# A graph-attention layer with the features as weights and the attention moving

## The chip, the cores and the metric

The kernel runs on one core of one Trainium2 chip. The metric is the device time of one execution in microseconds (us): the median of three runs of the kernel before. One further execution was taken with the hardware profiler; its trace is the source of every duration below. TensorE is called PE in the profile (PEld is its weight load), VectorE DVE, ScalarE ACT, GpSimd POOL, SyncE SP.

## What is computed

Four residual layers run over `x` of 32 batches x 512 nodes x 64 features, float32, with one 512x512 adjacency matrix `adj` for all batches. Each layer starts with `h = max(layernorm(x), 0)`:

- layer 0: `x += h Ws + (adj h) Wn + bias`
- layer 1: twice `z = relu((adj z) W_i)`, then `x += z`
- layer 2, graph attention, which the change is about:

```python
Wh = einsum('bnf,of->bno', h, W)
e1 = Wh @ a[:F_OUT]
e2 = Wh @ a[F_OUT:]
e = leaky_relu(e1[:, :, None] + e2[:, None, :], negative_slope=0.2)
att = softmax(where(adj > 0, e, -9e15), axis=-1)
x += elu(einsum('bij,bjo->bio', att, Wh))
```

- layer 3: attention with eight heads and an output layer of the same kind (`gat_layer`), again added to `x`.

## The kernel before

**Stages.** `x` stays on the chip, in 128 partitions of 4 blocks of nodes (C = 4, P = 128, F = 64). Layers 0, 1 and 2 are done in one software pipeline over M = 16 pairs of batches: a slot `k` (function `slot`) does layer 0 of pair k, layer 1 of pairs k-1 to k-3 and layer 2 of pairs k-3 to k-5. Seventeen slots run, then `drain` finishes the last four pairs of layer 2. After that layer 3 runs in periods of its own (`planned`), with other buffers; `drain` already starts its first features (`flow_period(-10)` to `(-2)`).

**Order.** For these layers the order of the instructions on TensorE, VectorE and ScalarE is exactly the order in which the code issues them (`manual_schedule`); each engine works through its own list and waits where something is missing. So what matters is what stands ahead of what in each list.

**Layer 2 of a pair** (class `Gat`) uses that exp(leaky_relu(e1 + e2)) is, up to a factor of the row that the softmax cancels, `max(exp(-0.8 e1), exp(0.8 e2)) * exp(0.2 e2)`.

- `flip` turns the normalised features with TensorE; `prepare` multiplies them by the weights (`wh_ps`, lines 960 to 971, with e2 as a 65th column) and makes e1 as a row in all partitions (`e1_ps`, L974); ScalarE takes the exponentials: into the last column of `v`, `q`, and `c` (L983 to L986).
- `weigh` (L991) multiplies the features by exp(0.2 e2) into `v`: 64 features and one column that will give the denominator.
- `scores` (L1000): VectorE makes `s = max(c, q) * mask`, eight instructions of 128x512 per pair, in two halves, four and four.
- `values` (L1014): TensorE multiplies, with `s` as weights and `v` (65 columns) as what moves. A block of `s` holds 64 neighbours of each of the two batches, one batch in partitions 0 to 63 and one in 64 to 127, so a product uses half the rows of the array, and the two halves go side by side. Per pair 4 x 8 x 2 = 64 products. A float32 product has two records in the trace, so 128 records; a transposition has one.
- `read` (L1029, L1030): VectorE takes the reciprocal of the 65th column and multiplies, straight from PSUM, into `o`.
- `rest`: ScalarE takes exp(o) (L1038), VectorE adds both parts of the elu to `x` (L1041, L1042), computes the mean and centres for layer 3's norm (L861 to L863), and ScalarE squares (L1044).

`end` is `read` and then `rest`.

**What stands around it in a slot.** TensorE's list at the end of a slot and the beginning of the next: `values`; the two projections of layer 0 (`po0`, L941); the second neighbour product of layer 1 (`nt1b`, L921); `judge`'s small transposition in slot 15; then, next slot, the first neighbour product of layer 1 (`nt1`, L921, of `hn`); `flip`; the projection `po1b` (L941), which needs the copy of `nt1b` by ScalarE (L928); layer 0's transposition and neighbour product; `prepare`; the projection `po1a`; `values`. ScalarE's list at that turn: exp(o) L1038, the square L1044, the copy of `nt1b`, the square of a norm (L881), the copies of `nt1` and of the flipped features (L312). VectorE's: the reciprocals of the norms and relu (L914, L885), then in some slots extra work (`begun`: `judge_rows`, seven instructions that judge one block of rows of the adjacency matrix, L201 to L213, in slots 6, 8, 10, 12; `judge` in slot 15; `edges`, which makes the mask, in slot 1; `scales`, in slot 4), then `read` and `rest`, then layer 0's addition to `x` (L1097), the next norms, `scores`.

The norms' spreads are summed by VectorE (L899) and turned into roots by ScalarE (`root`, L906), ahead of relu.

**Drain.** The pairs are called g2, g1, g0 and last. Products that lead nowhere (`fill`, L1168) stand in TensorE's list between the stages.

**Buffers.** `ps_t` has four PSUM buffers for everything tagged `ps`; `ps_g` two, for the `acc` of `values`; `ps_o` two, for projections.

Of the kernel before, what the change touches and what calls it, by code (L numbers as in the profile page):

```python
# [8 lines left out]
F32 = mybir.dt.float32  # L9
AF = mybir.ActivationFunctionType  # L10
OP = mybir.AluOpType
# [11 lines left out]
def fast_form(  # L23
# [201 lines left out]
    def halves(k):  # L225
        return slice(k * F, (k + 1) * F)

    def row_pair(name):

        return pairs_of[0].tile([P, 2, N], F32, name=name, tag="row")  # L230
# [611 lines left out]
    with (  # L842
# [107 lines left out]
        class Gat:  # L950
# [8 lines left out]
            def prepare(self):  # L959


                self.wh_ps = [
                    ps_t.tile([P, C, F + 1], F32, name="wh_ps", tag="ps") for b in range(2)
                ]
                for b in range(2 * C):
                    for k in range(2):
                        nc.tensor.matmul(
                            self.wh_ps[b // C][halves(k), b % C],
                            lhsT=self.ht[halves(k), b * F : (b + 1) * F],
                            rhs=wgv[halves(k), :], start=True, stop=True,  # L970
                        )
                e1 = ps_t.tile([P, N], F32, name="e1_ps", tag="ps")
                for k in range(2):
                    nc.tensor.matmul(  # L974
                        e1[halves(k), :], lhsT=wa1[halves(k), :F], rhs=self.ht[halves(k), :],
                        start=True, stop=True,
                    )
                self.v = work.tile([P, 2 * C, F + 1], F32, name="v")
                self.q = tiny.tile([P, 2 * C], F32, name="q")
                for b in range(2):  # L980
                    e2 = self.wh_ps[b][:, :, F]
                    some = slice(b * C, (b + 1) * C)
                    nc.scalar.activation(self.v[:, some, F], e2, AF.Exp, scale=0.2)  # L983
                    nc.scalar.activation(self.q[:, some], e2, AF.Exp, scale=0.8)
                self.c = row_pair("c")[:, 0]
                nc.scalar.activation(self.c, e1, AF.Exp, scale=-0.8)  # L986

            def weigh(self):
                for b in range(2):
                    v = self.v[:, b * C : (b + 1) * C]  # L990
                    nc.vector.tensor_tensor(  # L991
                        v[:, :, :F], self.wh_ps[b][:, :, :F],
                        v[:, :, F:].to_broadcast([P, C, F]), OP.mult,
                    )

            def scores(self, part):

                self.s = getattr(self, "s", []) + [row_pair("s") for b in range(C // 2)]
                for b in range(part * C, (part + 1) * C):
                    nc.vector.scalar_tensor_tensor(  # L1000
                        self.s[b // 2][:, b % 2], self.c, self.q[:, b : b + 1],
                        mask_t[b // C][:, b % C], op0=OP.max, op1=OP.mult,
                    )

            def values(self, rows=range(C)):

                if 0 in rows:
                    self.acc = [
                        ps_g.tile([P, C, F + 1], F32, name="acc") for k in range(2)
                    ]  # L1010
                for r in rows:
                    for b in range(2 * C):
                        for k in range(2):
                            nc.tensor.matmul(  # L1014
                                self.acc[k][:, r],
                                lhsT=self.s[b // 2][halves(k), b % 2, r * P : (r + 1) * P],
                                rhs=self.v[halves(k), b],
                                start=(b == 0), stop=(b == 2 * C - 1),
                            )

            def end(self):
                self.read()
                self.rest()

            def read(self):
                rec = tiny.tile([P, 2, C], F32, name="rec")
                self.sq = o = work.tile([P, 2, C, F], F32, name="o")
                for k in range(2):
                    nc.vector.reciprocal(rec[:, k], self.acc[k][:, :, F])  # L1029
                    nc.vector.tensor_tensor(  # L1030
                        o[:, k], self.acc[k][:, :, :F],
                        rec[:, k, :, None].to_broadcast([P, C, F]), OP.mult,
                    )

            def rest(self):
                o = self.sq
# [49 lines left out]
        def slot(k, more):  # L1086
            l0, l1 = 0 <= k < M, 0 <= k - 2 < M
            if l0:
                x2 = pair_of(k).rearrange("p k c f -> p (k c) f")
                nc.gpsimd.tensor_tensor(  # L1090
                    x2, x2, bias0_b[:, None, :].to_broadcast([P, 2 * C, F]), OP.add
                )
            if k - 3 in nt1b:
                nt1b[k - 3] = copied(nt1b[k - 3], "nt1b")
            if k - 1 in po0:
                x4 = pair_of(k - 1)
                nc.vector.tensor_tensor(  # L1097
                    x4, x4, po0.pop(k - 1).rearrange("p c k f -> p k c f"), OP.add
                )
            some = []  # L1100
            n = make(n1, k - 1)
            if n:
                n.a()
                n.square()
                some.append(n)
            if l1:
                h = n1.pop(k - 2).h
                nt1 = copied(neighbours(lambda c: h[:, c]), "nt1")
            if k - 4 in n2:
                gat[k - 4] = Gat(k - 4, n2.pop(k - 4).h)  # L1110
                gat[k - 4].flip()
            u = gat.pop(k - 5, None)
            if u:
                u.scores(0)
            if k - 3 in nt1b:
                ends(k - 3)
            if l0:
                h0 = n0.pop(k).h
                ht0 = flipped(h0, "ht0")
            n = make(n2, k - 3)  # L1120
            if n:
                n.a()
                n.square()
                some.append(n)
            if l0:
                nt0 = copied(neighbours(lambda c: h0[:, c]), "nt0")
            if u:
                u.scores(1)
            if k - 4 in gat:
                gat[k - 4].prepare()  # L1130
            if l1:
                z = middle(nt1)
            n = make(n0, k + 1)
            if n:
                n.a()
                n.square()
                some.append(n)
            some += ended
            ended.clear()
            s = Spread()  # L1140
            for n in some:
                s.add(n)
            if u:
                u.values()
            s.root()
            if k - 4 in gat:
                gat[k - 4].weigh()
            s.turn()
            for n in some:
                if isinstance(n, Gat):  # L1150
                    flow_stats[n.i] = n.mean, n.rstd
                else:
                    n.relu()
            if l0:
                po0[k] = project([(ht0, ws2), (nt0, wn2)], "po0")
            if l1:
                nt1b[k - 2] = neighbours(lambda c: z[:, c, :])
            if more:
                more()
            if u:  # L1160
                u.end()
# [8 lines left out]
        def drain():  # L1170
# [19 lines left out]
            s.add(u)  # L1190
            s.root()
            nt1b[M - 1] = copied(nt1b[M - 1], "nt1b")
            g2.values(range(C // 2))
            g1.weigh()
            s.turn()
            n.relu()
# [3 lines left out]
            n = make(n2, M - 1)  # L1200
            n.a()
            n.square()
            g2.values(range(C // 2, C))
            g1.scores(0)
            g0.flip()
            g2.read()
# [4 lines left out]
            s.add(n)  # L1211
            s.root()
            g1.values()
            s.turn()
            n.relu()
            last = Gat(M - 1, n2.pop(M - 1).h)
# [6 lines left out]
            g0.scores(1)  # L1223
            fill(6)
            g0.values()
            last.weigh()
            g1.rest()
            last.scores(0)
# [5 lines left out]
            last.scores(1)  # L1234
            fill(3)
            last.values()
            g0.rest()
            s.add(g1)
            last.read()
# [7 lines left out]
                flow_stats[n.i] = n.mean, n.rstd  # L1247


        mask_t = [  # L1250
            setup.tile([P, C, N], F32, name=f"mask{b}", tag=("raw", "mask")[b])
            for b in range(2)
        ]

        def edges():
            for b in range(2):
                for k in range(2):
                    blocks = mask_t[b][:, k::2]
                    nc.vector.tensor_scalar(
                        blocks[halves(k)], adj_t[halves(k), b * C // 2 : (b + 1) * C // 2],  # L1260
                        0.0, None, op0=OP.is_gt,
                    )
                    nc.sync.dma_start(blocks[halves(1 - k)], blocks[halves(k)])

        with tc.manual_schedule(
            engines={
# [609 lines left out]
```

## Time and profile before

| what | value |
|---|---|
| median of three runs | 2043.86 us (2043.75 to 2046.07) |
| the profiled execution's own time | 2045.32 us |
| its span in the trace | 2043.5 us |
| mean granted TensorE clock | 0.989 |
| PE busy 100 to 350 us | all of it |
| `values` of layer 2 (L1014), all 16 pairs | 2048 records, 124.0 us busy |
| its weight loads | 2048, 121.0 us busy |
| layers 0 to 2, end | 454 us (first product of layer 3's scores) |

How to read it: the profile's page has a line per engine, the span cut into 40 slices with the busy tenths of each engine and the granted clock (`PEclk`), and groups of instructions. A group's line gives line, engine, operation, output and inputs, the shape of the tile of the array (rows*columns) and of what moves, the count, then busy time and the mean duration in ns, then the idle time of the engine just before and what ended it. A line of the order of time gives the start, the length (to the modelled end), the engine, the line of code, the operation and its shapes, the count of instructions merged, and in brackets the idle time ahead of it with the engine and result that ended it. TensorE's instructions overlap, so the difference of two starts tells the pace and a duration does not.

### The profile page before, as it was taken

The page shows a single profiled execution, that of the slowest core. Times are in us where ns is not written, and L with a number is a line of the kernel's source. Part 1 is how long each engine was busy: PE and PEld are TensorE (multiplying, and loading weights), DVE is VectorE, ACT ScalarE, POOL GpSimd, SP SyncE. Part 2 cuts the span into 40 slices and gives each one's busy share as a digit, 9 for nine tenths or more (in the row PEclk, how much of TensorE's full clock was granted, in tenths as well). Part 3 has the DMA queues.
Part 4 walks back from the last instruction along what each step waited for, and adds up shares of the span by engine and source line. Part 5 has one row for each costly group of instructions (what it writes and reads, how often), then busy time and mean ns, then how long its engine had stood idle before and what let it go on. Part 6 is the DMA issues. An engine that isn't in the chain of part 4 may idle for free.

```text
span 2043.5 us, 32571 instructions
## 1 busy us (share of the span) xinstructions
PE 1980.7 (97%) x11038; PEld 811.0 (40%) x11038; DVE 1753.4 (86%) x4121; ACT 1295.2 (63%) x1960; POOL 1445.8 (71%) x834
## 2 busy tenths in 40 slices
PE   7999999997999999999999999999999999999995
PEld 4676676762333333333333333333333333333332
DVE  6699996768988899889898898888898898888984
ACT  3443443346677777777677777676676776766674
POOL 2000000006898989899999989898888988889996
PEclk9999999988999999999999999999999999999999
DMA  5000000002222323232332323333232323323233
GB/s 143 1 1 1 1 2 1 1 1 69 70 73 79 82 77 75 79 80 79 75 85 74 84 69 85 75 77 76 76 77 69 79 75 69 79 74 80 71 83 81
DMA packets 186464, 129.31 MB, mean 63 GB/s; under 512 B 125048, under 2 KB 130336, under 8 KB 186160
## 3 DMA queue, kind: packets, MB, share of 16 engines
q1 hardware_dynamic: 167056, 126.35, 23.9%
q10 hardware_dynamic: 18720, 0.59, 0.5%
q8 instruction: 89, 1.46, 0.3%
q14 instruction: 87, 0.71, 0.1%
q0 software_dynamic: 512, 0.20, 0.1%
HBM read 119.48 MB, written 5.37 MB: 61 GB/s over the span
## 4 chain that ended last, share of the span: by engine, by line
PE 57%; POOL 8%; DVE 4%; DMA 4%; ACT 2%; issue 2%; ACTq 0%; SPq 0%; POOLq 0%; DVEq 0%
PE s_ps L383 20%; PE av L438 19%; POOL p_att L416 6%; PE tot_ps L450 5%; PE y_ps L568 5%; PE gT_ps L613 4%; PE g_ps L550 3%; DMA topb<-top_row 2%; DVE p_att L395 2%; POOL p_att L420 2%; DVE p_att L432 1%; DMA top_row<-top 1%; PE hx_ps L310 1%; ACT e_ps L429 1%; DVE cat L586 1%
## 5 line engine op out<-in xcount | busy, mean ns | idle before, releaser
L416 POOL TENSOR_TENSOR p_att<-p_att,topb 128x1024 f32<-128x1024 f32 x429 | 1008.1, 2383 | 0.0
L395 DVE CUSTOM_DVE_ANT_0 p_att<-s_ps,flow_neg 128x512 f32<-128x512 f32 x1152 | 726.1, 686 | 91.2 <-PE s_ps L383 89.6
L383 PE MATMUL s_ps<-g,hx 64*128 64x512 f32 x2048 | 515.3, 613 | 16.6 <-DVE p_att L432 14.5
L420 POOL TENSOR_TENSOR p_att<-p_att,topb 128x512 f32<-128x512 f32 x286 | 360.5, 1282 | 170.5 <-DMA topb<-top_row 140.1
L429 ACT ACTIVATE p_att<-p_att 128x1024 f32<-128x1024 f32 x288 | 304.8, 1059 | 173.7 <-POOL p_att L420 91.1
L432 DVE TENSOR_TENSOR p_att<-e_ps,p_att 128x1024 f32<-128x1024 f32 x288 | 338.9, 1198 | 35.5 <-ACT e_ps L429 34.3
L429 ACT ACTIVATE e_ps<-p_att 128x1024 f32<-128x1024 f32 x288 | 293.1, 1029 | 88.1 <-POOL p_att L416 81.3
L383 PEld LDWEIGHTS s_ps<-g,hx 64*128 64x128 f32 x2048 | 174.8, 186 | 329.0 <-DVE top L395 173.8
L438 PE MATMUL av<-p_att,hd 128*64 128x512 f32 x1024 | 269.7, 605 | 0.0
L438 PE MATMUL av<-p_att,hn 128*64 128x512 f32 x1024 | 263.2, 592 | 0.0
L1090 POOL TENSOR_TENSOR x<-x,bias_b 128x512 f32<-128x512 f32 x16 | 20.3, 1274 | 280.3 <-DVE hn L863 280.3
L586 DVE SCALAR_TENSOR_TENSOR cat<-y_ps,bh,cat 128x512 f32<-128x512 f32 x256 | 180.1, 745 | 15.3 <-ACT cat L578 14.0
L562 ACT COPY g<-g_ps 128x512 f32<-128x512 f32 x128 | 131.8, 1138 | 81.1 <-PE g_ps L550 81.1
L578 ACT ACTIVATE cat<-y_ps,bh 128x512 f32<-128x512 f32 x256 | 161.4, 682 | 33.1 <-PE y_ps L568 32.2
L450 PE MATMUL tot_ps<-p_att,ones 128*32 128x512 f32 x1152 | 156.1, 607 | 4.0 <-DVE p_att L432 4.0
L568 PE MATMUL y_ps<-o_att,wh_sb 64*128 64x512 f32 x512 | 137.4, 594 | 0.0
L438 PEld LDWEIGHTS av<-p_att,hn 128*64 128x64 f32 x1024 | 73.7, 137 | 146.1 <-issue 146.1
L613 PE MATMUL gT_ps<-cat,wo_sb 128*64 128x512 f32 x512 | 131.6, 592 | 0.0
L438 PEld LDWEIGHTS av<-p_att,hd 128*64 128x64 f32 x1024 | 62.2, 136 | 165.4 <-issue 132.5
L1014 PE MATMUL acc<-v,s 64*128 64x65 f32 x2048 | 124.0, 280 | 0.7 <-DVE s L1000 0.4
L487 DVE TENSOR_TENSOR o_att<-av,recb 128x512 f32<-128x512 f32 x144 | 99.2, 689 | 29.4 <-DMA recb<-rec_row 26.8
L1014 PEld LDWEIGHTS acc<-v,s 64*128 64x128 f32 x2048 | 121.0, 194 | 5.9 <-DVE o L1030 1.2
(183 smaller groups left out, 2113.9 us busy)
## 6 DMA issues: line engine op xcount, KB each, us to landing
topb<-top_row SPq DMA_DIRECT2D x288, 256.0 KB
recb<-rec_row SPq DMA_DIRECT2D x288, 128.0 KB
out_dram<-y SPq DMA_DIRECT2D x32, 128.0 KB
x<-in_x_dram SPq DMA_DIRECT2D x3, 1024.0 KB
top_row<-top SPq DMA_DIRECT2D x144, 4.0 KB
parts<-tot SPq DMA_DIRECT2D x144, 4.0 KB
parts<-tot ACTq DMA_DIRECT2D x144, 4.0 KB
rec_row<-rec_flow SPq DMA_DIRECT2D x144, 4.0 KB
```

Source lines behind the costliest of these rows:

```text
L383: nc.tensor.matmul(ps[:, k], lhsT=x[halves(k), r * P : (r + 1) * P], rhs=g[halves(k), :], start=True, stop=True,)
L395: nc.vector.tensor_tensor_reduce(out=self.p[r][:, k], in0=ps[:, k], in1=flow_neg[:, r], scale=-1.0, scalar=BIG, op0=OP.add, op1=OP.min, ac ...
L416: engine.tensor_tensor(self.p[r], self.p[r], self.topb, OP.subtract)
L420: engine.tensor_tensor(p, p, self.topb[:, k], OP.subtract)
L429: nc.scalar.activation(to, self.p[r], AF.Exp, scale=-1.0)
L432: nc.vector.tensor_tensor(self.p[r], self.joined, self.p[r - 1], OP.add)
L438: nc.tensor.matmul(self.av[halves(k), :], lhsT=self.v(k, j) if j % 2 else self.less_next(k, j), rhs=self.p[j][:, k], start=(j == 0), stop= ...
L450: nc.tensor.matmul(ps[q : q + 32, :], lhsT=ones, rhs=self.p[2 * e + 1][:, k], start=True, stop=True,)
L568: nc.tensor.matmul(ps, lhsT=wh_sb[halves(k), 2 * self.i + k, :], rhs=self.o[halves(k), :], start=True, stop=True,)
L586: nc.vector.scalar_tensor_tensor(self.cat[:, k], self.y[k], bh[:, h : h + 1], self.cat[:, k], op0=OP.add, op1=OP.max,)
L613: nc.tensor.matmul(self.gps[halves(k), :], lhsT=wo_sb[:, h, :], rhs=Heads.cat.pop((self.b + k, h)), start=(h == 0), stop=(h == H - 1),)
L1014: nc.tensor.matmul(self.acc[k][:, r], lhsT=self.s[b // 2][halves(k), b % 2, r * P : (r + 1) * P], rhs=self.v[halves(k), b], start=(b == 0) ...
```

## The change

Layer 2 exchanges the roles of the operands in `values`. `v`, now of 128 neighbours of a single batch, is the weight, and `s` moves, 512 targets at a time; the output is the feature row by target, one batch in partitions 0 to 63 and one in 64 to 127. The denominators come from separate products: `v` carries 32 equal columns of exp(0.2 e2), and four products write to four groups of 32 partitions, two blocks of each batch, so that the sum over the groups is still to be made. New `keep` lets ScalarE copy both results out of PSUM. `read` then turns them back with TensorE: four products with a small matrix `pick` (two columns that add up the groups) give the denominators, four transpositions the features, and VectorE takes one reciprocal and one multiplication.

`prepare`, `weigh` and `scores` go over to blocks of one batch: e1 of each batch fills all 128 partitions, so there are two rows `c`; one mask serves both batches, and `edges` makes it in one instruction and without the four DMAs. `middle` (the projection po1a and its relu) is moved ahead of `prepare` in a slot. `drain` calls `keep` after each `values`, and does g2's `values` in one piece.

```diff
@@ prepare
-                for b in range(2 * C):
+                for c in range(C):
                     for k in range(2):
                         nc.tensor.matmul(
-                            self.wh_ps[b // C][halves(k), b % C],
-                            lhsT=self.ht[halves(k), b * F : (b + 1) * F],
+                            self.wh_ps[k][:, c],
+                            lhsT=self.ht[halves(k), c * P : (c + 1) * P],
                             rhs=wgv[halves(k), :], start=True, stop=True,
                         )
...
-                        e1[halves(k), :], lhsT=wa1[halves(k), :F], rhs=self.ht[halves(k), :],
+                        e1[k], lhsT=wa1[halves(k), :], rhs=self.ht[halves(k), :],
...
-                    nc.scalar.activation(self.v[:, some, F], e2, AF.Exp, scale=0.2)
+                    nc.scalar.activation(
+                        self.v[:, some, F:], e2[:, :, None].to_broadcast([P, C, 32]),
+                        AF.Exp, scale=0.2,
+                    )
...
-                nc.scalar.activation(self.c, e1, AF.Exp, scale=-0.8)
+                for k in range(2):
+                    nc.scalar.activation(self.c[:, k], e1[k], AF.Exp, scale=-0.8)
@@ values
-                for r in rows:
-                    for b in range(2 * C):
+                for c in range(C):
+                    for k in range(2):
+                        b = k * C + c
+                        nc.tensor.matmul(
+                            self.acc[halves(k), :], lhsT=self.v[:, b, :F],
+                            rhs=self.s[b // 2][:, b % 2],
+                            start=(c == 0), stop=(c == C - 1),
+                        )
+                for c in range(0, C, 2):
+                    for e in range(2):
                         for k in range(2):
+                            b, q = k * C + c + e, (2 * k + e) * 32
                             nc.tensor.matmul(
-                                self.acc[k][:, r],
-                                lhsT=self.s[b // 2][halves(k), b % 2, r * P : (r + 1) * P],
-                                rhs=self.v[halves(k), b],
-                                start=(b == 0), stop=(b == 2 * C - 1),
+                                self.tot[q : q + 32, :], lhsT=self.v[:, b, F:],
+                                rhs=self.s[b // 2][:, b % 2],
+                                start=(c == 0), stop=(c == C - 2),
                             )
+            def keep(self):
+                self.kept = []
+                for p in (self.acc, self.tot):
+                    t = work.tile([P, N], F32, name="kept")
+                    nc.scalar.copy(t, p)
+                    self.kept.append(t)
@@ read
+                acc, tot = self.kept
+                den = ps_g.tile([P, N], F32, name="den_ps", tag="acc")
+                den = den[:, : 2 * C].rearrange("p (c k) -> p c k", k=2)
+                for c in range(C):
+                    nc.tensor.matmul(
+                        den[:, c], lhsT=tot[:, c * P : (c + 1) * P], rhs=pick,
+                        start=True, stop=True,
+                    )
+                op = ps_t.tile([P, C, 2, F], F32, name="op_ps", tag="ps")
+                for c in range(C):
+                    nc.tensor.transpose(
+                        op[:, c].rearrange("p k f -> p (k f)"), acc[:, c * P : (c + 1) * P],
+                        ident,
+                    )
                 rec = tiny.tile([P, 2, C], F32, name="rec")
+                nc.vector.reciprocal(rec.rearrange("p k c -> p c k"), den)
                 self.sq = o = work.tile([P, 2, C, F], F32, name="o")
-                for k in range(2):
-                    nc.vector.reciprocal(rec[:, k], self.acc[k][:, :, F])
-                    nc.vector.tensor_tensor(
-                        o[:, k], self.acc[k][:, :, :F],
-                        rec[:, k, :, None].to_broadcast([P, C, F]), OP.mult,
-                    )
+                nc.vector.tensor_tensor(
+                    o, op.rearrange("p c k f -> p k c f"),
+                    rec[:, :, :, None].to_broadcast([P, 2, C, F]), OP.mult,
+                )
@@ slot
             if u:
                 u.scores(1)
+            if l1:
+                z = middle(nt1)
             if k - 4 in gat:
                 gat[k - 4].prepare()
-            if l1:
-                z = middle(nt1)
...
             if u:
                 u.values()
             s.root()
+            if u:
+                u.keep()
@@ drain
             g1.values()
+            g1.keep()
             s.turn()
...
             g0.values()
+            g0.keep()
             last.weigh()
             g1.rest()
...
             last.values()
+            last.keep()
             g0.rest()
@@ edges
+            nc.vector.tensor_scalar(mask_t, adj_t, 0.0, None, op0=OP.is_gt)
+            nc.vector.tensor_tensor(
+                pick, ident[:, 0::F], ident[:, 32::F], OP.add
+            )
```

In `slot`, `u.end()` (that is, `read` and `rest`) stays where it was: after `po0`, `nt1b` and the extra work.

## The prediction

> **What bounds the kernel now.** I read the page, then the order of time of the three engines in the stage that changes. Times are us from the start of the profiled execution.
>
> ```profile
> PE 1980.7 (97%) x11038; PEld 811.0 (40%) x11038; DVE 1753.4 (86%) x4121; ACT 1295.2 (63%) x1960; POOL 1445.8 (71%) x834
> PE   7999999997999999999999999999999999999995
> L1014 PE MATMUL acc<-v,s 64*128 64x65 f32 x2048 | 124.0, 280 | 0.7 <-DVE s L1000 0.4
> ```
>
> TensorE is busy in every slice. Layers 0 to 2 end near 454 us; the change is wholly ahead of that, so layer 3's 1590 us only start sooner or later. Now the steady slot (24.37 us, one pair of batches) on TensorE:
>
> ```profile
> 216.88 7.36 PE L1014 MATMUL acc<-v,s 64*128 64x65 f32 x128
> 224.18 0.49 PE L941 MATMUL po<-ws,ht 128*128 128x128 f32 x2
> ```
>
> The step that changes, `values`, takes 224.18 - 216.88 = **7.30**, with no idle time on TensorE. Every saving there looks like a gain, so the next view asks who is next late. It is the timeline of all engines at the turn of a slot:
>
> ```profile
> 227.61 0.17 DVE L1029 RECIPROCAL rec<-acc 128x4 f32<-128x4 f32 x1
> 228.82 0.69 DVE L1041 SCALAR_TENSOR_TENSOR x<-o,x 128x512 f32<-128x512 f32 x1
> 229.50 3.60 PE L921 MATMUL nt_ps<-adj_t,hn 128*128 128x512 f32 x8
> 231.27 0.69 DVE L863 TENSOR_TENSOR o<-x,mean 128x512 f32<-128x512 f32 x1
> 231.99 0.63 ACT L1044 ACTIVATE o<-o 128x512 f32<-128x512 f32 x1 [2.54 <-DVE o L863]
> 232.53 0.57 ACT L928 COPY nt1b<-nt_ps 128x512 f32<-128x512 f32 x1
> 233.37 1.06 PE L941 MATMUL po1b<-wl,nt1b 128*128 128x128 f32 x8
> ```
>
> Call N the moment at which TensorE starts the slot's first product (229.50). ScalarE works in order: the copy of nt1b stands behind the square of o, which waits for VectorE's chain from L1041. From L1041 to the copy's end are 233.10 - 228.82 = **4.28**; po1b, which needs the copy, comes up at N + **3.87**. So L1041 must start by N - 0.41; here it starts at N - 0.68, with 0.27 to spare. One slot later in the kernel, it was late already:
>
> ```profile
> 353.26 0.69 DVE L1041 SCALAR_TENSOR_TENSOR x<-o,x 128x512 f32<-128x512 f32 x1
> 356.98 0.57 ACT L928 COPY nt1b<-nt_ps 128x512 f32<-128x512 f32 x1
> 357.60 1.16 PE L941 MATMUL po1b<-wl,nt1b 128*128 128x128 f32 x8 [2.09 <-ACT nt1b L928]
> ```
>
> There N was 351.48, L1041 came at N + 1.78, and TensorE stood for 2.09 (1.78 + 0.41, within 0.1).
>
> **What the Trainium skill says.** "TensorE: Matmul & The Clock Gate", LDWEIGHTS (loading the stationary operand): the time goes with the columns of the weights, not their rows. The trace agrees: of 64x128 weights 128 took 7.30 (57 ns each, halves side by side), of 64x64 ones 32 took 0.98 (31 ns). So `values` is bound by its loads, and features as weights help. "TensorEngine Tiling (Array Packing)", When to Use Tiling, names this swap with column tiling for a narrow operand; layer 3 shows it below. The same page, PSUM Bottleneck: tiling doesn't speed up the evacuation. Here it is two more copies of 0.59. "TensorE: Matmul & The Clock Gate", What's actually happening: the clock is halved after an idle window of some 3.4 us. After the waits of 2.09 and 1.64 near 357 the granted clock was 0.50 in 362 to 364, so somewhat less idle time sufficed.
>
> **The change, on TensorE, per pair.** Layer 3 has the two new forms:
>
> ```profile
> 489.01 1.07 PE L450 MATMUL tot_ps<-p_att,ones 128*32 128x512 f32 x8
> 490.01 1.99 PE L383 MATMUL s_ps<-g,hx 64*128 64x512 f32 x8
> 492.83 1.03 PE L438 MATMUL av<-p_att,hn 128*64 128x512 f32 x4
> 493.69 1.03 PE L438 MATMUL av<-p_att,hd 128*64 128x512 f32 x4
> ```
>
> Four records of the 64-column form take 0.86; acc has 16: 3.44, and 0.05 for the change of form. Eight of the 32-column form take 1.00; the denominators have two such groups: 1.00 + 0.86 = 1.86. New `values`: **5.35**. `read` is new work here: four transposes, 0.44 (as ht_ps, 208.56 to 209.00), and eight records of 128x128 weights that move two columns. That form is shown once, in size_ps: two in 0.22, 0.11 each; m_ps's sixteen took 1.93, 0.12 each. The other end is 57 ns, the load pace of acc. I take 0.11: 0.90; the low end is 0.46. Sum: -7.30 + 5.35 + 0.90 + 0.44 = **-0.6** (low end -1.05). wh_ps has half the records with twice the columns (16 x 57 ns = 0.91 for 0.98), e1 twice the columns at the same 0.95: nothing.
>
> **What it moves.** The old reciprocal needed only `values`, which end 5.3 ahead of N. The new one needs products that stand behind po0 and nt1b in TensorE's order, and end at N + 0.15. Then o (0.69, from PSUM, one in place of four instructions) puts L1041 at N + **0.91**. The wait at po1b becomes 0.91 + 4.28 + 0.03 - 3.87 = **1.35** per slot, and behind po1b stands TensorE's whole slot. So a slot takes 24.37 - 0.6 + 1.35 = 25.12: +0.75. Ten slots (6 to 15) have it whole: **+7.5**. Slot 5 has only the gain: **-0.6**.
>
> **After judge_rows** (slots 6, 8, 10, 12) VectorE is later still. Its work from L1041 to relu's end was 21.15 (201.30 to 222.45), 1.07 of it waiting that falls away now (po1b, sq): relu ends at N + 21.0, judge_rows' 5.15 at N + 26.15. The next N is at N + 25.12, so the reciprocal starts 1.03 after it, L1041 at N + 1.95 (reciprocal 0.20, o 0.72): 1.04 later than above, four times: **+4.2**.
>
> **ScalarE.** Per pair one more exponential (0.6), two copies (1.1) and 128x128 for 128x4 outputs (0.31, the hs row, for 0.18, twice). In a slot the copies lie in the 7.7 that it waited ahead of L1038. In slot 4, with no old pair in flight, the square waits for the exponentials: 75.18 becomes about 76.0, and TensorE was waiting there (2.86, for VectorE's scales): **+0.85**.
>
> **Slot 16** (351.48 to 375.86) had waits of 2.09 and 1.64 and a halved clock. Now own_ps is no longer last, po1b waits 1.35, po1a for ScalarE's copy until N + 7.55, and the last scores arrive at N + 13.85: acc ends at 14.3, the denominators at 16.1, nt1b and read at 20.95 in place of 24.38. With 0.5 for the clock: **-2.9**.
>
> **The drain** (375.86 to 454) loses cover. The new `keep` stands ahead of the previous pair's `rest` in ScalarE's order. Before, its exponentials came early:
>
> ```profile
> 419.42 0.63 ACT L1038 ACTIVATE e<-o 128x512 f32<-128x512 f32 x1 [2.38 <-DVE o L1030]
> 439.80 0.61 ACT L1038 ACTIVATE e<-o 128x512 f32<-128x512 f32 x1
> ```
>
> Counted from 375.86 these are 43.6 and 63.9. Now g0's `values` (43.9 to 49.0, paced by scores) and two copies come first: the exponential at 50.1, the square at 53.1 for 49.9. Layer 3's first features stand behind it, 3.2 late; then hx, g (at half clock, after 8 us idle), read and fill: last's `values` run 69.5 to 74.9 (65.3 to 72.6 before). Copies to 76.1; only then g0's exponential, to 76.7; its remaining chain and the sum of squares, 3.0; last's reciprocal and o, 0.9; the 4.5 from L1041 to layer 3's first maximum: 85.1 against 79.3, where VectorE sets the pace: **+5.8**.
>
> **At nothing:** edges (VectorE 2.84 becomes about 1.2, in a slot where it waits 1.78 for ScalarE afterwards; four DMAs leave SP's queue, whose data nobody awaited at 84.7), pick (0.17), weigh and scores (same sizes), middle ahead of prepare (TensorE's sum is the same). PSUM: prepare now takes all four ps buffers; ScalarE's exponentials c free the two of e1 in time, except in the drain, where nt1b waits 1 us that later waits absorb.
>
> **Sum:** 0.85 - 0.6 + 7.5 + 4.2 - 2.9 + 5.8 = **+14.9**. The profiled execution took 2045.32 (span 2043.5): 2060. The median is 1.46 lower, so 2043.86 + 14.9 = **2059**. With the low end for the two-column products, the same steps give +11.
>
> **Rivals.** 0.2% is 4.1 us, about what a measurement of this kernel can tell from no change.
> *Forecast*, 0.57: the wait at po1b eats the saving; 2051 to 2065.
> *The clock falls too*, 0.12: waits of 2.4 after judge_rows halve the clock for 4 us each, 2 us lost: four times, 2067. For: 362 to 364. Against: the wait of 2.86 at 82 left the clock at 1.00.
> *Part of it*, 0.14: the po1b waits come, but VectorE makes up for judge_rows and the drain keeps its length, as its halved clock of 423 to 438 (g0's `values` took 13.8) disappears: -0.6 to +4.9, 2043 to 2049; 0.11 of it within 0.2%.
> *Faster*, 0.16: TensorE's saving stays. It decides at one place: L1041 at N - 0.41 or earlier, as when the turned-back products were issued ahead of nt1b, or ScalarE's nt1b copy ahead of the square. Then 16 pairs at -0.6 to -1.05: 2027 to 2034. The order written in the code speaks against it.
> *It does not do what it says*, 0.01: the column tiles run one after the other, 16 + 16 records of 0.43 in place of 5.35: +8.4 per pair, 2180. The 0.86 above excludes it nearly.
>
> Faster 0.16; within 0.2% 0.11; slower 0.57 + 0.12 + 0.03 + 0.01 = 0.73. The range of 2041 to 2068 leaves out the faster case and little above; the forecast's own is 2051 to 2065.
>
> **What would show it.** `values` near 5.35 and read near 1.35 per pair; the idle time ahead of po1b `<-ACT nt1b` of 1.3 to 2.5 in slots 6 to 15, where there was none; slots of 25.1; L1041 0.9 after N; in the drain the exponentials behind the copies. The forecast is wrong if po1b shows no idle time, or slots are shorter than 24.37.

## The result and the profile after

The changed kernel takes **2077.43 us** (median of four runs, 2077.38 to 2078.57) against 2043.80 for the kernel before, run beside it: a ratio of 1.0163, interval 1.0146 to 1.0181. It is slower by 33.6 where 15 were forecast. Its profiled execution took 2077.38 (span 2075.5, mean granted clock 0.985), 32.1 more than that of before. Line numbers below are those of the changed kernel: `values` L1018 (features) and L1027 (denominators), `keep` L1037, `read` L1049 to L1062, `rest` L1070 to L1076.

The first lines of the page after, busy time and TensorE's 40 slices:

```profile
PE 1984.1 (96%) x9438; PEld 744.5 (36%) x9438; DVE 1746.2 (84%) x4087; ACT 1319.3 (64%) x2008; POOL 1446.3 (70%) x834
PE   7999999877999999999999999999999999999995
```

TensorE's busy time hardly moved (1980.7 before), though it has 1600 records fewer. The page shows where it stands: the eighth to tenth slice (363 to 519 us), which read 997 before, read 877. One step down in the order of time, the steady slot of the changed kernel; read it from the turn of the slot (N is the start of the `nt_ps` product at 211.85):

```profile
210.57 0.95 PE L1049 MATMUL den_ps<-pick,kept 128*128 128x2 f32 x8
211.85 3.60 PE L921 MATMUL nt_ps<-adj_t,hn 128*128 128x512 f32 x8
212.78 0.69 DVE L1073 SCALAR_TENSOR_TENSOR x<-o,x 128x512 f32<-128x512 f32 x1
215.95 0.63 ACT L1076 ACTIVATE o<-o 128x512 f32<-128x512 f32 x1 [2.54 <-DVE o L863]
216.49 0.57 ACT L928 COPY nt1b<-nt_ps 128x512 f32<-128x512 f32 x1
217.11 1.16 PE L941 MATMUL po1b<-wl,nt1b 128*128 128x128 f32 x8 [1.22 <-ACT nt1b L928]
225.44 3.65 PE L1018 MATMUL acc<-s,v 128*64 128x512 f32 x16
229.03 1.92 PE L1027 MATMUL den<-s,v 128*32 128x512 f32 x16
230.88 0.49 PE L941 MATMUL po<-ws,ht 128*128 128x128 f32 x2
```

`values` fell to 230.88 - 225.44 = 5.44 and `read` costs 211.85 - 210.57 = 1.28 on TensorE. Then the chain of the forecast: VectorE's L1073 starts at N + 0.93, the square of o follows, the copy of nt1b stands behind the square, and po1b waits 1.22. There are 12 such waits in the layers 0 to 2, 16.4 us together; there was one before.

By stage (N6 is the start of slot 6, and so on; the last column is the sum of the forecast's own terms):

| stretch | before | after | moved | forecast |
|---|---|---|---|---|
| start to N6 | 107.39 | 108.47 | +1.1 | +0.25 |
| N6 to N16, ten slots | 244.09 | 258.13 | +14.0 | +11.7 |
| slot 16 | 24.38 | 22.24 | -2.1 | -2.9 |
| drain: its N to layer 3's first maximum (VectorE, L395) | 79.32 | 101.13 | **+21.8** | +5.8 |
| from there to the end of the execution's own time | 1590.1 | 1587.4 | -2.7 | 0 |

The first row says little of the change: four of the kernels below differ from one another only in the drain (the change, all keeps behind rest, no fill, g0's keep behind rest), and they reach N6 between 107.8 and 110.4. So positions can be off by two or three us from the start alone; stretches leave it out.

Two thirds of the loss are in the drain. In TensorE's order of time there, after:

```profile
400.03 5.40 PE L921 MATMUL nt_ps<-adj_t,z 128*128 128x512 f32 x8 [1.93 <-ACT c L990]
418.01 2.07 PE L974 MATMUL e_ps<-ht,wa 64*128 64x512 f32 x2 [0.41 <-DVE o L1062]
420.02 4.95 PE L1202 MATMUL fill_ps<-adj_t,ident 128*128 128x512 f32 x6
424.90 3.65 PE L1018 MATMUL acc<-s,v 128*64 128x512 f32 x16
437.65 1.81 PE L974 MATMUL e_ps<-ht,wa 64*128 64x512 f32 x2 [3.04 <-ACT c L990]
439.61 7.97 PE L1202 MATMUL fill_ps<-adj_t,ident 128*128 128x512 f32 x12
447.50 3.65 PE L1018 MATMUL acc<-s,v 128*64 128x512 f32 x16
463.10 2.21 PE L310 MATMUL hx_ps<-ident,hs 128*128 128x128 f32 x8 [10.09 <-ACT hs L524]
470.59 5.18 PE L1202 MATMUL fill_ps<-adj_t,ident 128*128 128x512 f32 x6
```

Three things are to be seen. The second e1 product (`e_ps`) waits, once for ScalarE's `c`, the exponential that reads the first one; nt1b waits for `c` too, and runs at half clock after it (5.40 for 3.60). `fill` stands directly ahead of each `values` and, in part at a low clock, takes 4.95, 7.97 and 5.18, where 2.84, 5.42 and 3.8 stood before. And TensorE stands 10.09 ahead of layer 3's first features, where it did not wait before (432.73). The chain that ended last, of the changed kernel, runs through every one of these fills (start, length, what):

```profile
420.09 4.88 PE fill_ps L1202 x6
424.97 3.58 PE acc L1018 x16
439.61 7.97 PE fill_ps L1202 x12
447.57 3.58 PE acc L1018 x16
470.80 4.97 PE fill_ps L1202 x6
```

Before, g1's `values` began 26.8 after the drain's N, g0's 43.0 and last's 65.3; now 36.1, 58.7 and 86.9. The two exponentials shown of before are those of g1 (419.42, 43.6 after N) and g0 (439.80, 63.9). The profile of after has them at 453.56 and 481.76, so 64.7 and 92.9 after N, where 50.1 and some 76 were forecast.

The steady slot shows the same shortage of buffers in small. TensorE and ScalarE around `e_ps` of the changed kernel:

```profile
223.23 0.63 ACT L881 ACTIVATE sq<-hn 128x512 f32<-128x512 f32 x1 [2.89 <-DVE hn L863]
223.77 0.57 ACT L928 COPY nt<-nt_ps 128x512 f32<-128x512 f32 x1
223.90 1.61 PE L974 MATMUL e_ps<-ht,wa 64*128 64x512 f32 x4
224.39 0.29 PEld L974 LDWEIGHTS e_ps<-ht,wa 64*128 64x128 f32 x2 [0.24 <-ACT nt L928]
```

Between its two halves `e_ps` waits until ScalarE's copy of nt0 frees the fourth `ps` buffer, and that copy stands behind a square that waits for VectorE. From 223.90 to `values` at 225.44 are 1.54 where 0.95 were reckoned.

### The profile page after: what moved, and what is told of

Its sections match the earlier page's. It is cut to its first block, busy times and chain, and to the rows that moved or that the text cites. A ratio compares the mean times of both kernels' runs of the same rounds, so it can differ in the third digit from the quotient of the medians.

```text
span 2075.5 us, 29392 instructions
## 1 busy us (share of the span) xinstructions
PE 1984.1 (96%) x9438; PEld 744.5 (36%) x9438; DVE 1746.2 (84%) x4087; ACT 1319.3 (64%) x2008; POOL 1446.3 (70%) x834
## 4 chain that ended last, share of the span: by engine, by line
PE 78%; DVE 11%; POOL 5%; ACT 3%; DMA 2%; issue 2%; ACTq 0%; SPq 0%; DVEq 0%; POOLq 0%
PE s_ps L383 23%; PE av L438 21%; PE tot_ps L450 6%; PE y_ps L568 5%; PE gT_ps L613 5%; PE nt_ps L921 5%; POOL p_att L416 3%; PE g_ps L550 3%; PE acc L1018 2%; DVE s L1005 2%; PE den L1027 1%; DVE mean L861 1%; PE hx_ps L310 1%; PE po L941 1%; DVE p_att L395 1%
## 5 line engine op out<-in xcount | busy, mean ns | idle before, releaser
L395 DVE CUSTOM_DVE_ANT_0 p_att<-s_ps,flow_neg 128x512 f32<-128x512 f32 x1152 | 726.0, 686 | 100.0 <-PE s_ps L383 98.2
L568 PE MATMUL y_ps<-o_att,wh_sb 64*128 64x512 f32 x512 | 137.0, 594 | 0.0
L921 PE MATMUL nt_ps<-adj_t,hn 128*128 128x512 f32 x256 | 117.0, 600 | 0.8 <-DVE hn L885 0.8
L528 POOL TENSOR_TENSOR hd<-hn 128x128 f32<-128x128 f32 x32 | 15.6, 487 | 138.5 <-ACT hn L519 138.5
```

Of the source, the lines that this page charges most:

```text
L395: nc.vector.tensor_tensor_reduce(out=self.p[r][:, k], in0=ps[:, k], in1=flow_neg[:, r], scale=-1.0, scalar=BIG, op0=OP.add, op1=OP.min, ac ...
L568: nc.tensor.matmul(ps, lhsT=wh_sb[halves(k), 2 * self.i + k, :], rhs=self.o[halves(k), :], start=True, stop=True,)
L921: nc.tensor.matmul(p, lhsT=lhs(k), rhs=adj_t[:, k, :], start=(k == 0), stop=(k == C - 1))
```

## The experiments

**My theory** after the result: the slots are long because the products of `read` come behind nt1b (as forecast), and two more things are dear beyond the forecast: prepare's second e1 product has no free buffer, and the drain's fill no longer lies in idle time. **Rivals:** the order of keep against the previous pair's exponential makes the drain (the forecast's own step); the drain is long only because the slots hand it late work; the waits cost clock.

All ratios are to the kernel before on the same chip; positions and stretches are of one profiled execution of each kernel. "Stretch" is from the drain's last po1b to layer 3's first maximum.

| kernel | ratio, interval | last po1b | stretch | first maximum |
|---|---|---|---|---|
| before | 1 | 391.8 | 63.4 | 455.2 |
| the change | 1.0163 (1.0146 to 1.0181) | 410.8 | 79.2 | 490.0 |
| products ahead | 1.0078 (1.0060 to 1.0095) | 393.1 | 78.9 | 472.0 |
| square later | 1.0156 (1.0139 to 1.0173) | 411.3 | 78.8 | 490.1 |
| all keeps behind rest | 1.0158 (1.0141 to 1.0175) | 410.2 | 79.4 | 489.6 |
| no fill | 1.0137 (1.0112 to 1.0161) | 411.2 | 69.1 | 480.3 |
| e1 in po | 1.0118 (1.0100 to 1.0136) | 405.7 | 73.3 | 478.9 |
| old slots, new drain | 1.0099 (1.0076 to 1.0123) | 403.3 | 77.0 | 480.3 |
| new slots, old drain | 1.0082 (1.0066 to 1.0099) | 407.6 | 63.4 | 471.0 |
| products ahead, e1 in po, old drain | 1.0000 (0.9991 to 1.0008) | 388.8 | 63.4 | 452.1 |
| before, no fill | 0.9989 (0.9980 to 0.9998) | 392.1 | 60.4 | 452.5 |
| e1 in po, no fill | 1.0100 (1.0086 to 1.0115) | 405.4 | 68.0 | 473.4 |
| products ahead, e1 in po | 1.0019 (1.0010 to 1.0027) | 389.4 | 74.7 | 464.1 |
| ... and g0's keep behind rest, no fill | 1.0001 (0.9993 to 1.0010) | 388.7 | 63.9 | 452.7 |
| g0's keep behind rest | 1.0139 (1.0122 to 1.0155) | 412.9 | 75.8 | 488.7 |
| products ahead, e1 in po, g0's keep behind rest | 1.0011 (1.0002 to 1.0020) | 388.8 | 71.1 | 459.9 |

### Products ahead of nt1b

```diff
-            def read(self):
+            def back(self):
                 acc, tot = self.kept
...
                 po0[k] = project([(ht0, ws2), (nt0, wn2)], "po0")
+            if u:
+                u.back()
             if l1:
```

`back` holds the eight products and four transpositions; `read` keeps the reciprocal and the multiplication. In the drain both stay together.

> The changed kernel with one step moved: the products that turn the result back (den_ps, op_ps) are issued on TensorE between po0 and nt1b instead of behind nt1b, and in the drain where read stood; VectorE's part of read stays where it is. Theory of the order (the wait at po1b comes from read standing behind nt1b, and all of VectorE's and ScalarE's later work of the slot is late with it, the copy that e1's second product waits for too): L1041 comes some 3.4 us earlier, the idle time ahead of po1b (16.4 us in all) falls below 4, e1 takes 0.95 again in place of 1.54, slots fall from 25.8 to 23.8 to 24.3, and the time to about 2055. Rival (the slots are longer because TensorE and ScalarE have more work or a lower clock): the waits only move elsewhere, slots stay above 25.3 and the time above 2072.

The waits at po1b are gone but for 0.43 in every slot that follows judge_rows and 1.83 in slot 16; slots are 24.21 to 24.26, some 23.6. The second e1 product was expected to stop waiting too, but `e_ps` still takes 1.54 in every second slot. In the kernel with the products ahead:

```profile
232.93 1.16 PE L941 MATMUL po1b<-wl,nt1b 128*128 128x128 f32 x8 [0.43 <-ACT nt1b L928]
```

The drain's first po1b comes at 376.6, 17.5 earlier than with the change, and its stretch is the same 78.9. So the wait of the forecast is the cause of the slots' loss, and the drain is a matter of its own.

### The square later

```diff
             if n:
                 n.a()
-                n.square()
-                some.append(n)
             if l0:
                 nt0 = copied(neighbours(lambda c: h0[:, c]), "nt0")
+            if n:
+                n.square()
+                some.append(n)
```

> The changed kernel with one ScalarE instruction moved: the square of layer 2's norm (L881) is issued behind the copy of nt0 instead of ahead of it. Theory (e1's second product stands 0.6 us per slot for a PSUM buffer that ScalarE's copy of nt0 frees, and that copy stands behind the square, which waits for VectorE): e_ps falls from 1.54 to 0.95 in the ten full slots, slots by 0.6, the time by about 6 to 2071. Rival (e1 takes 1.54 because the 128-column form of its weights is slower, or because of the clock): e_ps stays at 1.54 and the time within 1 us of 2077.

The copy of nt0 no longer waits for the square, and `e_ps` falls to 1.01: the buffer is the cause of its wait. But nothing is won. After judge_rows VectorE sets the pace, so what TensorE saves comes back at po1b (2.20 for 1.66):

```profile
224.76 1.08 PE L974 MATMUL e_ps<-ht,wa 64*128 64x512 f32 x4
244.05 1.16 PE L941 MATMUL po1b<-wl,nt1b 128*128 128x128 f32 x8 [2.20 <-ACT nt1b L928]
```

Two slots together went from 51.70 to 51.18, but one slot took 1.7 more (26.79, with the neighbour product after its wait at half clock, 4.97) and slot 16 took 1.8 more: there the granted clock was 0.50 from 374 to 380, and `e_ps` took 2.02. The expected 6 were wrong.

### All keeps behind the previous pair's rest

`g1.keep()`, `g0.keep()` and `last.keep()` moved behind `g2.rest()`, `g1.rest()` and `g0.rest()`.

> The changed kernel with the drain's ScalarE order changed: keep of g1, g0 and last is issued behind the rest of the pair before it (g2, g1, g0) instead of ahead of it. Theory of the order (keep ahead of rest lengthens the drain): the exponential of g1's rest comes some 10 us earlier, but layer 3's first features still stand behind g0's two copies, so they gain only about 3; the last pair's rest no longer follows g0's; together 4 to 7 us, 2070 to 2073. Rival (the drain's 21.7 us come from PSUM waits, fill and the halved clock, and the order of keep is worth little): within 2 us of 2077.

The rival was right for the sum, not for the reason. Moving g1's copies made TensorE wait for them, ahead of everything that g0 needs, and that ate what the earlier exponential gave (10.09 to 6.53 ahead of the features):

```profile
436.88 1.87 PE L1049 MATMUL den_ps<-pick,kept 128*128 128x2 f32 x8 [6.66 <-ACT kept L1037]
463.02 2.21 PE L310 MATMUL hx_ps<-ident,hs 128*128 128x128 f32 x8 [6.53 <-ACT hs L524]
```

### No fill

All four `fill` calls of the drain left out; their products are used nowhere.

> The changed kernel without the four fills of the drain (the products that lead nowhere; the output does not depend on them). Rival of the order (fill stood in time in which TensorE would have waited before; now values, which is shorter, waits for fill itself): each fill that stands ahead of values goes from the path, 4 to 14 us faster, 2063 to 2073. Theory of the clock (the drain is long since TensorE's clock is halved, and fill holds it up): the values of the drain run at half clock throughout, 5.4 us more each, and the time is 2077 to 2090.

The first maximum comes 9.7 earlier, though `values` now run at half clock: g0's features took 6.21 for 3.65. The whole time doesn't tell it apart from the change (the intervals overlap). Layer 3's first products run at a low clock then and take 1.2 of the lead back by its first output projection (y_ps, L568: 529.2 for 537.7); by the last one 1.8 of it are left, and what takes the rest is not shown.

### The second e1 product in another pool

```diff
-                e1 = [ps_t.tile([P, N], F32, name="e1_ps", tag="ps") for k in range(2)]
+                e1 = [
+                    ps_t.tile([P, N], F32, name="e1_ps", tag="ps"),
+                    ps_o.tile([P, N], F32, name="e1_ps", tag="po"),
+                ]
```

> The second e1 product writes into the pool of po1a and po0 instead of a ps buffer; nothing else moves. Theory (four ps buffers are too few for prepare): e_ps takes 1.0 in place of 1.54, the slots that don't follow judge_rows fall from 25.63 to about 25.1, those after it stay at 26.07 because there VectorE sets the pace; in the drain the wait of 3.04 at e_ps goes. First maximum of layer 3 at 484 to 487 (489.97 with the change), whole time +27 to +30 against before. Rival (the second e1 product waits for something else, for instance for its weights or for the order of ScalarE): e_ps stays near 1.5 and the first maximum near 490.

`e_ps` takes 1.01 in every slot, and slots are 25.10 and 26.08 as expected. The drain gained more than I thought (478.9 where 484 to 487 were expected): its first po1b comes 2.5 earlier, the first maximum 11.0, so 8.5 lie in the drain. nt1b at its start waits 0.98 for ScalarE's z and keeps its clock. The wait of 3.04 at `e_ps` did not go as expected: it moved to the fill behind it, which takes a `ps` buffer too. In TensorE's order of time of this kernel (`values` is L1021 and fill L1205 here):

```profile
396.60 3.70 PE L921 MATMUL nt_ps<-adj_t,z 128*128 128x512 f32 x8 [0.98 <-ACT z L1118]
400.23 3.65 PE L1021 MATMUL acc<-s,v 128*64 128x512 f32 x16
429.60 8.42 PE L1205 MATMUL fill_ps<-adj_t,ident 128*128 128x512 f32 x12 [3.04 <-ACT c L993]
```

From the drain's first po1b to that `values` are 8.6 (391.62 to 400.23); with the change 11.3 (394.10 to 405.36). Of the 5.9 in the stretch, 2.9 lie ahead of g1's `values` (`e_ps` and fill take 5.4 in place of 8.4), 1.5 ahead of g0's, and 1.5 in the fill ahead of last's, at a better clock (3.7 for 5.2). One buffer, **11.0** in all (11.6 counted from the start of slot 6, as this execution began 0.6 later), some of it by way of the clock.

### Half the pipeline in each form

A second class `Old` holds the `prepare` to `read` of the kernel before, with masks of its own in bytes:

```diff
+        def form(i, h):
+            return (Old if i < M - 4 else Gat)(i, h)
```

and the same with `i >= M - 4`, with the old order in the drain. The last four pairs thus have one form and the first twelve (the expectations say thirteen) the other.

> Old form of the attention for the first thirteen pairs (finished in the slots), new form for the last four pairs (finished in the drain); both masks are made. Theory (the change costs the slots some 12 and the drain some 20, independently): slots of 24.4 as before, the drain's start as before at about 376 to 377, first maximum near 475 to 478, whole time +19 to +23. Rival (the drain is long only because the slots hand it late work): first maximum near 460, whole time under +8.

> New form for the first thirteen pairs, old form and old order of the drain for the last four. Theory: slots of 25.6 and 26.1 as with the change, the drain's start at about 388, then 79 as before: first maximum at 466 to 470, whole time +11 to +15. Rival (late slots make the drain long): first maximum over 478, whole time over +22.

The old drain behind new, late slots has a stretch of 63.4, to 0.1 that of before: what makes the drain long is the new form in it, not what comes ahead. The new drain behind old slots has 77.0. (In that kernel slot 16 took 28.4 for 22.1 from one po1b to the next, its `values` at half clock; its whole time belongs to neither theory.)

### Both remedies of the slots, old drain

Products ahead, the second e1 product in the other pool, and the old form for the last four pairs: the best that the parts suggested.

> New form for the first thirteen pairs with the turned-back products ahead of nt1b and the second e1 product in the pool of po1a; old form and order in the drain. Theory: no po1b wait over 0.5 except in slot 16, slots of 23.1 to 24.2, the drain's start near 370, first maximum at 447 to 453 against 455.2 before: whole time -2 to -8. Rival (once TensorE is relieved, VectorE with judge_rows sets 24.2 for every slot, and what is won is given back): first maximum within 2 of 455, whole time within 0.2%.

The slots are 23.6 to 23.7, and 24.2 after judge_rows (24.37 before), and layers 0 to 2 end 3.0 earlier. The whole time is that of before: 13 runs against 17, ratio 1.0000. The rival was half right: in every second slot VectorE with judge_rows sets 24.2. Where layer 3 loses the 3.0 is not settled; counted at its output projection (y_ps, L568) the lead is 2.4 at its first product and gone after a third of layer 3. Part of it may lie between executions: before has a median of 2047.8 beside this kernel, on another chip than its own profiled execution of 2045.3, and the rest of the time after the first maximum, which no edit touches, is 1587 to 1597 in the executions shown here.

### The fill, before and after

> The kernel before without its fill products in the drain; they compute nothing that is used. Theory (in the kernel before they lie in time in which TensorE would wait for scores, so they cost little and keep the clock): first maximum of layer 3 at 453 to 460 against 455.2, whole time within 6 of before. Rival (they are as dear there as with the change, so they are no cost of the change): first maximum at 445 or less.

> The change with the second e1 product in the pool of po1a, and without the fill products. Theory (buffers and fill are two separate pieces of the drain's 21.8): first maximum at 469 to 474, that is 5 to 10 below 478.9 with the fill, whole time +18 to +24. Rival (both took the same idle time): not below 477.

Before, fill costs next to nothing: without it the first maximum comes 2.7 earlier, but the old `values` of g0 and last take 14.43 and 13.85 at half clock (g0's took 13.8 with fill too), and layer 3's first y_ps comes at 502.1 for 502.4. With the change it costs more: beside the freed buffer its removal brings the stretch from 73.3 to 68.0, and the first y_ps from 527.2 to 522.1. The features of the new `values` lose 1.7 to 2.6 at half clock (6.25 for 3.65 in last), the old ones of last 6.5 (13.85 for 7.36); so in the old drain the clock gave back what fill costs, to 0.3 at the first y_ps, and in the new one it does not. In the whole time the intervals with and without fill (1.0118 and 1.0100) overlap.

### Both remedies, new drain; and the order of one pair

> The change with the turned-back products ahead of nt1b and the second e1 product in the pool of po1a, the new form in the drain too. Theory (the two causes add): slots of 23.7 and 24.2, first maximum at 459 to 463 (472.0 with the first alone, 478.9 with the second alone), whole time +5 to +10. Rival (one cause hides the other): first maximum over 466, whole time over +12.

The two causes nearly add: 464.1 for 459 to 463, with slots of 23.7 and 24.2. The last po1b comes 2.4 earlier than before and the stretch is 11.3 longer: what is left, +0.19%, is the drain.

> The kernel with both edits, and in the drain the copies of keep for the pair g0 behind the exponential of g1, and no fill products. Theory (the drain's length is ScalarE's order and the fill): features of layer 3 start some 3 earlier, first maximum at 446 to 455, whole time -6 to +3. Rival (what is taken from ScalarE's chain is given back at half clock): first maximum over 457, whole time over +4.

> The change with one pair's order turned round in the drain: the copies of keep for g0 stand behind the exponential and the square of g1; every other copy stays where the change has it. Theory (keep ahead of the previous pair's exponential is a piece of the drain's 21.8, as forecast, and moving g1's copies as well in the earlier experiment hid it): the wait of 10.1 ahead of layer 3's first features falls to about 6.5, the first maximum to 484 to 487 against 489.97. Rival (the order is worth nothing in any pair): within 1 of 490.

> Both edits of the buffers and of the products, and the same turn of one pair's order, with the fill products left in. Theory (order and fill are separate pieces): first maximum at 459 to 461 against 464.1, so that some 7 or 8 of the 11.4 by which the version without fill was shorter belong to the fill; whole time +2 to +5. Rival (the order gave nearly all of it): first maximum at 455 or less.

The edit in these three is `g0.keep()` behind `g1.rest()`, one pair alone. In the changed kernel the wait ahead of the features falls from 10.09 to

```profile
461.76 2.21 PE L310 MATMUL hx_ps<-ident,hs 128*128 128x128 f32 x8 [6.53 <-ACT hs L524]
```

and the stretch from 79.2 to 75.8 (the first maximum only from 490.0 to 488.7, as this run reached slot 6 some 2 later). With the other edits it falls from 74.7 to 71.1. So the order is worth 3.4 to 3.6, and taking the fill away another 7.2 (71.1 to 63.9). With everything mended the new form in all pairs is level with before (1.0001). But this version has no fill; beside before without fill (0.9989) it is 0.1% slower, with intervals that just overlap.

## Why the prediction was wrong in size

**Right: direction and mechanism of the slots.** `values` 5.44 (5.35), read 1.28 (1.34), L1073 at N + 0.93 (0.91), po1b's wait 1.22 (1.35), a slot 25.63 (25.12). Putting the products ahead of nt1b took the waits away. After judge_rows the wait was 1.66, not 2.39: the slot had grown by the 0.6 of `e_ps`, so VectorE was that much less late.

**Wrong: "PSUM: ... ScalarE's exponentials c free the two of e1 in time, except in the drain, where nt1b waits 1 us that later waits absorb".** I had counted the buffers and seen all four in use, and then put the cost at nothing without asking who frees the fourth one. It is ScalarE's copy of nt0, behind a square that waits for VectorE: 0.6 in each full slot. And in the drain later waits did not absorb it: nt1b waits 1.93, on the chain that ended last, and the second e1 product waits 3.04 ahead of g0's `values`. Measured: 11.0 of the 18.7 that the forecast lacked (33.6 - 14.9), 2.5 ahead of the drain (about as much as the +14.0 of the ten slots is above the forecast) and 8.5 in it.

**Wrong: the drain's +5.8, "paced by scores".** I let g0's `values` start when VectorE had its scores and so took fill as hidden ahead of them, as it was before. It is on the path now: 5.3 to 7.2. The term that I did name, the copies ahead of the exponential, is real: 3.4 to 3.6. The g2 `values`, now in one piece ahead of the last po1b, is 5.44 where 3.72 stood (391.78 - 388.06 before): 1.7, not named. Nor was the wait at the drain's own first po1b (1.22), which comes 5.26 after N for 3.87: 1.4. Sum, with buffer, fill and order each taken away after the one before: 8.5 + 5.3 + 3.4 + 1.7 + 1.4 = 20.3, or 22.2 with the larger fill; measured 21.8. But not all of the fill's share is new: without fill the old stretch is 3.0 shorter as well (63.4 to 60.4). If that is taken off, 17.3 to 19.2 are accounted for at the first maximum and 2.6 to 4.5 stay unexplained.

**Up to slot 6** 1.1 were measured where 0.25 were forecast: TensorE waited 3.57 just ahead of slot 5 (2.86 before), the granted clock was 0.50 from 84 to 86, and slot 5's first neighbour product took 5.11 for 3.60. But kernels that are alike up to there reach N6 2.6 apart, so this can't be told from the start of the execution. Slot 16 came within 0.8 of the forecast.

**The rivals.** "Faster" was said to be decided by the products' place. The place did decide the slots, from 25.6 to 24.2 and 23.6; but 2027 to 2034 did not come: with the products ahead the kernel still took 1.0078 of before. TensorE's saving is worth 0.65 to 0.75 only in slots without judge_rows and 0.15 in the others, and even with both remedies and the old drain the kernel is only level with before. "The clock falls too" was not it in the slots: the waits of 1.66 left the next neighbour product at 3.60.

## What to carry to other kernels

When a change lets a step take the last free buffer of a pool, name the instruction that frees the next one and what that instruction waits for on its own engine; "freed in time" is a term of the sum like any other. Filler products are worth what the clock saves on the work behind them: when that work gets shorter, work the filler out anew, its own need of a buffer included. And in a drain, where little other work covers a wait, cost each new hand-over between engines by its chain and not with the slack of the steady slot.

## What the hardware showed

The clock falls earlier than I expected. "TensorE: Matmul & The Clock Gate", What's actually happening, in the Trainium skill, gives an idle window of some 3.4; here a wait of 1.93 (with one of 1.22 six us ahead of it) was followed by a neighbour product of 5.40 for 3.60, while one of 0.98 left it at 3.70 and the waits of 1.66 in the slots left it at 3.60. Of twelve waits of 2.2 after judge_rows, in three of the kernels above, one was followed by the half clock (4.97) and eleven were not. In slot 16, waits of 1.22 and 1.09 some 2 us apart left `e_ps` at 1.08 with the change and were followed by 2.02 with the square later. The section also says that the window runs freely, whatever the kernel does; that would fit such differences, and no run here shows it. So a stretch with waits that come to about 2 has to be reckoned at both clocks.
